# A tanh recurrence, attention and routed experts on one core: unused TensorE products at the start, chunk 0's steps on VectorE, and a planner that keeps the steps' rhythm

## The chip, the cores and the metric

The kernel runs on one core of one Trainium2 chip. A core has TensorE (matrix products, written to eight PSUM banks), VectorE, ScalarE and GpSimd, and a queue SP that only issues DMAs. In the profile they are PE (with PEld for loading weights), DVE, ACT, POOL and SP. Each engine takes its instructions in the order in which the program lists them, and waits on semaphores for the others. The metric is the device time of one execution in microseconds (us), lower is better, as a median over runs.

## The reference, cut to what matters

There are 4 sequences of 1024 tokens with 256 channels; all arithmetic is float32. A first block normalises the rows, makes two projections, and runs a recurrence along the tokens:

```python
px = x @ W_state.T + b_state;  g = sigmoid(x @ W_gate.T + b_gate)
state = tanh(p_t + state);  out_t = g_t * state        # one token after the other
x = x + layernorm(outs)
```

A second block normalises again, does causal attention with 16 heads of 16 channels (queries and keys RMS-normalised per head), adds it, RMS-normalises, picks the best two of four experts per token and adds their weighted outputs:

```python
attn = softmax(where(causal, q @ k.T * HD ** -0.5, -inf));  x = x + attn @ v @ wo.T
wts = top-2 of softmax(x_norm @ gate_w.T), renormalised
moe = wts[:, 0:1]*o0 + wts[:, 1:2]*o1 + wts[:, 2:3]*o2 + wts[:, 3:4]*o3
```

The block's result is normalised and added to x.

## The kernel before, in words

The tokens are cut into NI = 8 chunks of 128 tokens, each with all four sequences (B = 4). Per chunk there are these pieces of work:

- `inputs` (line 491) loads the rows into one of two buffers `xc`, on SP.
- `projections` normalises them (statistics in lines 448 and 449, the reciprocal root by `newton`, lines 432 to 439, or for chunk 0 by GpSimd's power in line 424; scaling in line 520), transposes them (line 462, copies from PSUM in line 471) and multiplies by the weights in four tiles of 128x512, eight products in line 533. VectorE evicts the tiles: states in line 551, halves of the gates in line 547.
- `recurrence` is one chain of 1024 steps for all chunks, 8 columns (2 halves of the channels x 4 sequences) wide. GpSimd adds the last state (line 582), ScalarE takes the tanh (line 585; line 578 for the very first).
- `gates` takes the tanh of the gates (line 566), after the chunk before has finished its steps.
- `before` multiplies gates and states in two parts, after step 96 and after step 128 (line 614), transposes (line 622), normalises, adds the input, stores it (line 651), normalises again and transposes; `heads` makes queries, keys and values (lines 710, 777, 797).
- Attention goes in tiles (i, b), chunk i and sequence b, with i + 1 blocks of keys for each of 16 heads: scores in two layouts (line 882), maxima on VectorE (line 974), exponentials on ScalarE (line 1023), masks on GpSimd (line 1043), sums (line 1064), output projection, and the router. It needs chunk i's recurrence, and grows with i.
- The experts follow when all tiles are done (lines 1504, 1523, 1564).

The order is written by a planner within the program. Each piece of work is a generator that yields an `Op` (engine, assumed cost, priority, events to wait for, slots, banks). `Plan.run` repeatedly takes the `Op` that can start first by its assumed clocks (ties by priority) and writes its instructions next on its engine. So the assumed costs (0.21 us for a sum and for a tanh) fix the order, and the chip then runs this order at its own pace. `projections` may go ahead for the first AT_ONCE = 5 chunks; later ones wait until the attention of chunk 0 is done. `once` holds the constants: memsets, masks, the scaling of weights by norms, zeros in DRAM. `fill` writes unused products (line 416) on TensorE wherever the plan has a gap of 0.8 us between 60 and 420 us of planned time.

Of the kernel before, what the change touches and what calls it, by code (L numbers as in the profile page):

```python
# [18 lines left out]
P = 128  # L19
# [23 lines left out]
def kernel(  # L43
# [42 lines left out]
    hb_g = const.tile([P, NCC], F32, name="hb_g")  # L86
    nc.vector.tensor_scalar_mul(hb_g, vec[:, 6:8], 0.5)

# [8 lines left out]
    for arena, group in (  # L97
# [18 lines left out]
    sandwich(  # L116
        tc, ident, mhalf, hb_g, route, keys, values,
        x, w_sg, w_qk, w_v, w_o, w_gate, row_d, weights, e_weights, out,
# [18 lines left out]

AT_ONCE = 5

# [31 lines left out]
class Op:  # L171
    def __init__(self, eng, cost, prio, reads=(), slots=(), banks=0, lag=0.0, either=(), ahead=0.0):
        self.eng, self.cost, self.prio, self.reads = eng, cost, prio, reads
        self.slots, self.banks, self.lag, self.either = slots, banks, lag, either
        self.ahead = ahead


class Plan:
# [7 lines left out]
    def __init__(self, banks):  # L186
# [4 lines left out]
        self.fill = None  # L191

    def ev(self, *key):
        return self.events.setdefault(key, Ready())

    def start(self, op):
        t = self.clock[op.eng]
        for r in op.reads:
            t = max(t, r.at + self.HOP)
        if op.either:  # L200
            t = max(t, min(r.at for r in op.either) + self.HOP)
        for s in op.slots:
            t = max(t, s.best()[1])
        for b in self.banks.pick(op.banks):
            t = max(t, self.banks.free[b])
        return t

# [11 lines left out]
    def run(self, streams):  # L219
        waiting = {}  # L220
        for n, s in enumerate(streams):
            op = next(s, None)
            if op is not None:
                waiting[n] = op
        while waiting:
            best = None
            for n, op in waiting.items():
                t = self.start(op)
                key = (t - op.ahead, op.prio, n)
                if best is None or key < best[0]:  # L230
                    best = (key, n, op, t)
            _, n, op, t = best
            assert t < float("inf"), "streams wait for each other"
            if op.eng == "PE" and op.cost and self.fill:
                self.fill(t)
            got = []
            for s in op.slots:
                k, _ = s.best()
                s.free[k] = float("inf")
                got.append((s, k))  # L240
            for b in self.banks.pick(op.banks):
                self.banks.free[b] = float("inf")
                got.append(b)
            self.clock[op.eng] = t + op.cost
            self.end = t + op.cost + op.lag
            try:
                waiting[n] = streams[n].send(got)
            except StopIteration:
                del waiting[n]
# [3 lines left out]
def sandwich(  # L253
    ctx, tc, ident, mhalf, hb_g, route, keys, values,
    x, w_sg, w_qk, w_v, w_o, w_gate, row_d, weights, e_weights, out,
# [75 lines left out]
    def once():  # L331

        yield Op("SP", 2.0, 50.0, [ev("x", 0)], lag=8.0)
        for t, ap in loads:
            nc.sync.dma_start(t, ap)
        done("loaded")
        yield Op("DVE", 2.0, 50.0, [ev("st", 0)])
        nc.vector.tensor_copy(ident_h, ident)
        nc.vector.memset(av, 0.0)
# [14 lines left out]
        for k in range(11):  # L354
# [3 lines left out]
            )  # L358
        for p in pads.tiles:
            yield Op("DVE", 1.2, 50.0)  # L360


            nc.vector.memset(p, 0.0)
            nc.vector.memset(p[:, 1, :, HD : HD + 1], 1.0)
        for cc in range(NCC):
# [10 lines left out]
        for e in range(1, E):  # L376
            nc.vector.memset(low[:, e, :e], 1.0)
            nc.vector.memset(nlow[:, e, :e], 0.0)
        yield Op("POOL", 1.5, -1.0)
        nc.gpsimd.memset(mask, 0.0)  # L380
        nc.gpsimd.affine_select(
            out=mask, in_=mask, pattern=[[-1, P]],
            compare_op=ALU.is_ge, fill=NEG, base=0, channel_multiplier=1,
        )
        nc.gpsimd.memset(late[:, : 3 * P], 0.0)

        nc.gpsimd.memset(earlier, 1.0)
# [5 lines left out]
        for k in range(KINDS):  # L393
# [8 lines left out]
            allow_small_or_imprecise_dtypes=True,  # L402
        )
        done("once")

    def fill(until):

        now = plan.clock["PE"]
        if not FILLED[0] <= now <= FILLED[1] or until - now < LEAST:
            return  # L410
        k, = banks.pick(1)
        if banks.free[k] > now:
            return
        n = int((until - now - 0.4) / 0.35)
        for _ in range(n):
            nc.tensor.matmul(banks.tiles[k], lhsT=ident_h, rhs=late, start=True, stop=True)
        banks.free[k] = max(banks.free[k], now + 0.35 * n)
# [9 lines left out]
    def newton(z, tag):  # L427

        n = z.shape[1]
        y = stat.tile([P, n], F32, tag=tag + "y", name=tag + "y", bufs=1)  # L430
        t = stat.tile([P, n], F32, tag=tag + "t", name=tag + "t", bufs=1)
        nc.vector.tensor_scalar(
            y.bitcast(I32), z.bitcast(I32), -0.5, float(0x5F3759DF), ALU.mult, ALU.add
        )
        nc.vector.tensor_scalar(z, z, -0.5, None, ALU.mult)
        for _ in range(3):
            nc.vector.tensor_tensor(t, y, y, ALU.mult)
            nc.vector.tensor_tensor(t, t, z, ALU.mult)
            nc.vector.scalar_tensor_tensor(y, t, 1.5, y, ALU.add, ALU.mult)
        return y  # L440

    def moments(prio, tiles, tag, reads):

        mv = stat.tile([P, len(tiles), 2], F32, tag=tag, name=tag)
        for n, t in enumerate(tiles):
            yield Op("DVE", 0.6, prio, reads)
            st6 = stat.tile([P, 6], F32, tag="st6", name="st6")
# [3 lines left out]

    def transposed(prio, srcs, reads, name, ahead=0.0):

# [13 lines left out]
        for cc, (eng, copy) in enumerate(  # L467
            (("ACT", nc.scalar.copy), ("DVE", nc.vector.tensor_copy))
        ):
            yield Op(eng, 0.65, prio, [ev(name, "in PSUM")])  # L470
            copy(to[:, cc, : n * P], banks.tiles[bs[cc]][:, : n * P])  # L471
            give(bs[cc])
# [7 lines left out]
    def states(i):  # L480

        both = keys.rearrange("p b (h t) -> p (b h) t", h=NHC)[:, :, i * P : (i + 1) * P]
        return both[:, : NCC * B, :], both[:, NCC * B :, :]

    def inputs():
# [9 lines left out]
    def projections():  # L495


        for i in range(NI):
            prio = 4.0 * i - 8.0
            while i not in xc_of:  # L500
                yield Op("DVE", 0.0, prio, [ev("x", i)])
            x_c = xcs.tiles[xc_of[i][1]]
            x_rows = [x_c[:, b, :] for b in range(B)]
            mv = yield from moments(
                prio, x_rows, "mv0", [ev("x", i), *([ev("av", B - 1)] if i >= AT_ONCE else [])]
            )
            done("mv0", i)
            z = stat.tile([P, B], F32, tag="z0", name="z0")
            if i:
                yield Op("DVE", 2.2, prio)  # L510
                nc.vector.tensor_scalar(z, mv[:, :, 1], LN_EPS, None, ALU.add)
                r = newton(z, "r0")
            else:
# [4 lines left out]
            for b in range(B):  # L518
                yield Op("DVE", 0.35, prio, [ev("r0", i)])
                nc.vector.tensor_scalar(  # L520
                    x_rows[b], x_rows[b], mv[:, b, 0:1], r[:, b : b + 1],
                    ALU.subtract, ALU.mult,
                )
            done("ln", i)
            to, lnT_ = yield from transposed(prio, x_rows, [ev("ln", i)], f"lnT{i}")
            give(xc_of[i])
            lnT = big.tiles[to[1]]
            st, g = states(i)
            for half, dc in ((0, 0), (0, 1), (1, 0), (1, 1)):
# [14 lines left out]
                pb = pb.rearrange("p (b t) -> p b t", b=B)  # L544
                yield Op("DVE", 0.68, prio, [ev("pp", i, half, dc)])
                if half:
                    nc.vector.tensor_scalar(
                        tile, pb, 0.5, hb_g[:, dc : dc + 1], ALU.mult, ALU.add
                    )
                else:  # L550
                    nc.vector.tensor_scalar(tile, pb, b_s[:, dc : dc + 1], None, ALU.add)
                give(pp)
                if (half, dc) == (0, 1):
                    done("st", i)
            done("half g", i)
# [13 lines left out]
    def recurrence():  # L569

        prev = None
        for i in range(NI):
            st, _ = states(i)
            last = ev("st", i)
            for t in range(P):
                if prev is None:
                    yield Op("ACT", 0.21, -9.0, [last])
                    nc.scalar.activation(st[:, :, t], st[:, :, t], AF.Tanh)
                else:
                    yield Op("POOL", 0.21, -9.0, [last])  # L580
                    s = sp.tile([P, NCC * B], F32, tag="s", name="s")
                    nc.gpsimd.tensor_tensor(s, st[:, :, t], prev, ALU.add)  # L582
                    done("s")
                    yield Op("ACT", 0.21, -9.0, [ev("s")])
                    nc.scalar.activation(st[:, :, t], s, AF.Tanh)  # L585
# [5 lines left out]
                if t == MOST - 1:  # L591
                    done("most", i)
            done("rec", i)


# [722 lines left out]
    def gate(pr, w, sm):  # L1318
# [31 lines left out]
    plan.run([  # L1350
        inputs(), projections(), gates(), once(), recurrence(), before(),
        *(heads(0, [b]) for b in range(B)), scores(), look_maxima(),
# [382 lines left out]
```

## Time and profile before

| | us |
|---|---|
| median of 3 runs (lowest, highest) | 1473.57 (1470.53, 1474.31) |
| the profiled execution's own time | 1475.52 |
| its span, first to last instruction | 1473.8 |
| PE busy | 1324.7 (90%) |
| DVE busy | 897.8 (61%) |
| ACT busy | 709.1 (48%) |
| POOL busy | 466.0 (32%) |

The profile is of one execution. A row of the timeline gives start, busy time, engine, line, operation, output and inputs with shapes, how many were merged, and in brackets the idle time of the engine before it and who ended it. A row of the stages gives a stretch of the span and, for every engine, its busy time and number of instructions in it, and the clock that TensorE was granted as a share of full speed. Line numbers below are those of the kernel before; the changed kernel's have shifted.

### The profile page before, as it was taken

Reading aid. Unit: us, or ns where it says so; the run is one execution under the profiler, and the core shown is the slowest. Engines: PE = TensorE matmul, PEld = TensorE weight load, DVE = VectorE, ACT = ScalarE, POOL = GpSimd, SP = SyncE. Lnnn points to the kernel's source line nnn. Section 1 sums busy time; section 2 is a strip of 40 time slices with the busy share of each in tenths; the row PEclk is TensorE's granted clock in tenths of the full one; section 3 lists DMA queues with packets and bytes.
Section 4 is the critical chain, followed back from the end, with each engine's and each line's share of the span. In section 5 each row is a group of like instructions: output and inputs, shape, how many; then the busy total and the mean of one; then the engine's idle time right before and its main releaser. Section 6 shows DMA issues by size and latency. Waiting matters only on the chain. (4 is left out here: it accounts for less than half of the span.)

```text
span 1473.8 us, 43265 instructions
## 1 busy us (share of the span) xinstructions
PE 1324.7 (90%) x17491; PEld 1032.5 (70%) x17506; DVE 897.8 (61%) x2725; ACT 709.1 (48%) x2144; POOL 466.0 (32%) x1466
## 2 busy tenths in 40 slices
PE   4578788998998999999999999999899999999994
PEld 2235446666676776787677677887688889888883
DVE  5566578599688788778877887783414312123331
ACT  2445555655765765776665455657122222223220
POOL 2433544534444444334311100111223312114221
PEclk8789899999999989998999999999899999999997
DMA  4010010001000010001000100221222110102100
GB/s 127 26 46 2 2 43 16 17 2 46 3 31 16 3 32 17 3 18 31 3 4 18 31 3 4 68 75 61 63 76 65 54 50 29 37 23 80 53 28 23
DMA packets 35847, 48.96 MB, mean 33 GB/s; under 512 B 7702, under 2 KB 27926, under 8 KB 35606
## 3 DMA queue, kind: packets, MB, share of 16 engines
q1 hardware_dynamic: 28774, 25.20, 5.5%
q0 software_dynamic: 6560, 20.09, 4.8%
q8 instruction: 143, 2.34, 0.7%
q14 instruction: 98, 0.80, 0.2%
q10 hardware_dynamic: 272, 0.52, 0.1%
HBM read 32.34 MB, written 13.73 MB: 31 GB/s over the span
## 5 line engine op out<-in xcount | busy, mean ns | idle before, releaser
L1023 ACT ACTIVATE ex<-bank 128x512 f32<-128x512 f32 (+1 forms) x592 | 326.2, 582 | 152.1 <-PE bank L882 87.2
L882 PE MATMUL bank<-keys,q 32*128 32x128 f32 x4608 | 352.7, 293 | 16.4 <-ACT q L761 3.6
L582 POOL TENSOR_TENSOR s<-keys 128x8 f32<-128x8 f32 x1023 | 223.1, 218 | 384.5 <-ACT keys L585 373.6
L882 PE MATMUL bank<-q,keys 32*128 32x128 f32 x4608 | 334.7, 293 | 6.5 <-ACT ex L1023 4.1
L882 PEld LDWEIGHTS bank<-q,keys 32*128 32x128 f32 x4608 | 273.7, 193 | 77.1 <-issue 42.9
L585 ACT ACTIVATE keys<-s 128x8 f32<-128x8 f32 x1023 | 218.5, 214 | 211.7 <-POOL s L582 209.1
L882 PEld LDWEIGHTS bank<-keys,q 32*128 32x128 f32 x4608 | 293.0, 193 | 35.9 <-DVE nm L974 6.0
L974 DVE TENSOR_REDUCE nm<-bank 128x1 f32<-128x512 f32 (+4 forms) x336 | 203.2, 639 | 51.4 <-PE bank L882 42.9
L967 DVE CUSTOM_DVE_ANT_0 bank<-bank,late 128x512 f32<-128x512 f32 (+2 forms) x320 | 188.4, 623 | 50.2 <-PE bank L882 49.0
L1043 POOL TENSOR_SCALAR_AFFINE_SELECT ex<-ex 128x256 f32<-128x256 f32 (+1 forms) x240 | 102.7, 429 | 261.6 <-ACT ex L1023 260.7
L1064 PE MATMUL av<-ex,values 128*17 128x128 f32 x4608 | 175.1, 282 | 2.2 <-DVE avT L1083 1.1
L1504 PE MATMUL bank<-values,keys 128*128 128x256 f32 x632 | 150.3, 385 | 6.2 <-PEq L1668 3.2
L1064 PEld LDWEIGHTS av<-ex,values 128*17 128x17 f32 x4608 | 110.0, 99 | 39.1 <-issue 15.2
L1504 PEld LDWEIGHTS bank<-values,keys 128*128 128x128 f32 x632 | 119.5, 193 | 23.8 <-issue 3.7
L1564 ACT ACTIVATE keys<-bank 128x256 f32<-128x256 f32 x136 | 52.2, 384 | 156.1 <-PE bank L1504 155.6
L1504 PE MATMUL bank<-keys 128*128 128x256 f32 x384 | 84.8, 379 | 0.0
L1504 PEld LDWEIGHTS bank<-keys 128*128 128x128 f32 x384 | 73.0, 190 | 9.9
L1591 DVE SCALAR_TENSOR_TENSOR rwnext<-av,rwnext 128x192 f32<-128x192 f32 x28 | 10.4, 414 | 101.6 <-PE av L1523 101.6
L533 PE MATMUL bank<-big,wsg 128*128 128x512 f32 x128 | 63.7, 643 | 5.9 <-ACT big L471 5.9
L710 PE MATMUL bank<-wqk,big 128*128 128x512 f32 x128 | 65.2, 638 | 3.2 <-ACT big L471 3.2
L1523 PE MATMUL av<-keys 128*128 128x192 f32 x384 | 66.4, 326 | 0.0
L1564 ACT ACTIVATE hid<-bank 128x256 f32<-128x256 f32 x66 | 25.4, 384 | 85.2 <-PE bank L1504 85.2
(238 smaller groups left out, 1720.2 us busy)
## 6 DMA issues: line engine op xcount, KB each, us to landing
row_d<-xn SPq DMA_DIRECT2D x16, 512.0 KB
xn<-in_x SPq DMA_DIRECT2D x8, 512.0 KB
xc<-in_x SPq DMA_DIRECT2D x7, 512.0 KB
keys<-in_e_l SPq DMA_DIRECT2D x2, 1024.0 KB
keys<-in_e_w SPq DMA_DIRECT2D x2, 512.0 KB
keys<-in_e_down SPq DMA_DIRECT2D x2, 384.0 KB
rwnext<-row_d,ids POOLq DMA_INDIRECT x36, 4.0
xc<-in_x SPq DMA_DIRECT2D x4, 128.0 KB
```

The costliest lines, as they stand in the source:

```text
L582: nc.gpsimd.tensor_tensor(s, st[:, :, t], prev, ALU.add)
L585: nc.scalar.activation(st[:, :, t], s, AF.Tanh)
L710: nc.tensor.matmul(pqk, lhsT=hT[:, cc, b * P : (b + 1) * P], rhs=wqk[:, cc, :], start=(cc == 0), stop=(cc == NCC - 1),)
L882: nc.tensor.matmul(banks.tiles[pbs[j]][:, m * P : (m + 1) * P], lhsT=k if kind == "sT" else q, rhs=q if kind == "sT" else k, start=(m == 0 ...
L967: nc.vector.tensor_tensor_reduce(out=s_, in0=s_, in1=late[:, 4 * P - w :], scale=-1.0, scalar=FMAX, op0=ALU.add, op1=ALU.min, accum_out=by ...
L974: nc.vector.tensor_reduce(by_slot[:, half, h0:h1, 2 * p + j], banks.tiles[pb][:, m0 * P : m1 * P].rearrange("p (h w) -> p h w", h=h1 - h0) ...
L1023: nc.scalar.activation(exs.tiles[ex[1]][:, j, : step.w], banks.tiles[pb][:, : step.w], AF.Exp)
L1043: nc.gpsimd.affine_select(out=d, in_=d, pattern=pattern, compare_op=ALU.is_ge, fill=0.0, base=0, channel_multiplier=-1,)
L1064: nc.tensor.matmul(av[32 * j : 32 * j + HD + 1, hc, :], lhsT=v_all[:, b, kb, 4 * hc + j, :], rhs=exs.tiles[ex[j // 2][1]][:, j % 2, m * P ...
L1504: nc.tensor.matmul(hb[0].tiles[hb[1]], lhsT=w[:, j, m * P : (m + 1) * P], rhs=src[:, j, :], start=(j == 0), stop=(j == nk - 1),)
L1523: nc.tensor.matmul(ob[0].tiles[ob[1]][:, t, :], lhsT=src[:, j, t * P : (t + 1) * P], rhs=w[:, j, :], start=(j == 0), stop=(j == nk - 1),)
L1564: nc.scalar.activation(to, src, AF.Gelu)
```

## The change

- At the start VectorE makes a bfloat16 identity, and TensorE multiplies it by itself BEFORE_ALL = 100 times into a bank that nobody reads, ahead of chunk 0's transposes.
- Chunk 0's two state tiles are evicted in two pieces each, the first 32 steps apart from the other 96. The first tanh waits for the first piece of the second tile.
- Chunk 0's sums (BY_VECTOR = 1) are done by VectorE instead of GpSimd.
- Projections of chunks 1 and 2 are cut into small VectorE instructions (`small`): statistics per 128 columns, scaling per 128 columns, copies and evictions of 128 columns, each an `Op` of its own. Chunks 3 and 4 no longer go ahead (AT_ONCE = 3).
- GpSimd writes the masks first, and the pads that VectorE cleared before.
- The planner's costs for a step are 0.24 (GpSimd) or 0.17 (VectorE) and 0.22 (ScalarE) instead of 0.21 and 0.21, and an `Op` that would delay the next step's `Op` on its engine is put behind it, unless it is too long for any gap and can start right behind the last step.

Cut to its core:

```diff
-AT_ONCE = 5
+SOONEST = 32
+BEFORE_ALL = 100
+BY_VECTOR = 1
+FITS = 0.05
+RIGHT_BEHIND = 0.06
+AT_ONCE = 3
...
+        if op.eng in self.chain and not op.every and op.cost:
+            ended, due, cost = self.chain[op.eng]
+            if t < due < t + op.cost - FITS and not (
+                op.cost > due - ended and t <= ended + RIGHT_BEHIND
+            ):
+                t = due + cost
         return t
...
+            if op.every:
+                self.chain[op.eng] = t + op.cost, t + op.every, op.cost
...
+    def begin():
+        yield Op("DVE", 0.2, -20.0)
+        nc.vector.tensor_copy(ident_h, ident)
+        done("ident")
+        pb, = yield Op("PE", 6.5, -20.0, [ev("ident")], banks=1)
+        for _ in range(BEFORE_ALL):
+            nc.tensor.matmul(
+                banks.tiles[pb][:, :P], lhsT=ident_h, rhs=ident_h, start=True, stop=True
+            )
+        give(pb)
+        yield Op("DVE", 0.2, -7.5, [ev("r0", 0)])
+        nc.vector.tensor_scalar_mul(hb_g, vec[:, 6:8], 0.5)
+        done("hb")
...
+            small = 0 < i < AT_ONCE
...
-                yield Op("DVE", 0.68, prio, [ev("pp", i, half, dc)])
...
+                pieces = [(slice(0, B), slice(0, P))]
+                if small:
+                    pieces = [(slice(b, b + 1), slice(0, P)) for b in range(B)]
+                elif i == 0 and not half:
+                    pieces = [(slice(0, B), slice(0, SOONEST)), (slice(0, B), slice(SOONEST, P))]
+                for k, (bs, ts) in enumerate(pieces):
+                    yield Op("DVE", 0.68 / len(pieces) + 0.05, prio, [ev("pp", i, half, dc)])
...
+                    if (half, dc, k) == (0, 1, 0):
+                        done("st", i)
...
-                    yield Op("POOL", 0.21, -9.0, [last])
+                    eng, name, cost = (
+                        (nc.vector, "DVE", 0.17) if i < BY_VECTOR else (nc.gpsimd, "POOL", 0.24)
+                    )
+                    step = 0.28 + cost
+                    if t == 0:
+                        plan.chain.clear()
+                    yield Op(name, cost, -9.0, [last], every=step)
                     s = sp.tile([P, NCC * B], F32, tag="s", name="s")
-                    nc.gpsimd.tensor_tensor(s, st[:, :, t], prev, ALU.add)
+                    eng.tensor_tensor(s, st[:, :, t], prev, ALU.add)
                     done("s")
-                    yield Op("ACT", 0.21, -9.0, [ev("s")])
+                    yield Op("ACT", 0.22, -9.0, [ev("s")], every=step)
...
-        for p in pads.tiles:
-            yield Op("DVE", 1.2, 50.0)
-            nc.vector.memset(p, 0.0)
-            nc.vector.memset(p[:, 1, :, HD : HD + 1], 1.0)
...
+        for p in pads.tiles:
+            yield Op("POOL", 1.6, 50.0, [ev("st", 0)])
+            nc.gpsimd.memset(p, 0.0)
+            nc.gpsimd.memset(p[:, 1, :, HD : HD + 1], 1.0)
```

## The prediction

> **What bounds the kernel now.** The page's table of 40 slices came first: TensorE is 90% busy over the span and low only in the first tenth and the last slice. Then busy time by stage, cut where each chunk's recurrence ends (line 622 starts 0.1 to 1.5 us behind that). Columns: stretch, length, busy time (count) of PE, PEld, DVE, ACT, POOL, granted clock, DMA share, GB/s.
>
> ```profile
> 17.90:88.60 70.70, 40.78 (x103) 18.71 (x102) 42.58 (x161) 29.38 (x132) 28.93 (x142) 0.76 0.11 34
> 88.60:171.80 83.20, 66.50 (x573) 40.45 (x580) 51.81 (x169) 45.73 (x171) 37.44 (x145) 0.89 0.06 17
> 171.80:247.30 75.50, 59.89 (x441) 39.10 (x445) 58.84 (x199) 40.02 (x160) 30.46 (x133) 0.93 0.10 29
> 247.30:340.30 93.00, 87.09 (x1240) 60.90 (x1239) 71.42 (x214) 57.25 (x204) 46.46 (x174) 0.98 0.06 19
> 740.60:1010.00 269.40, 262.75 (x6136) 208.45 (x6132) 212.49 (x574) 155.36 (x311) 33.81 (x78) 0.99 0.11 35
> 1010.00:1473.80 463.80, 427.72 (x2512) 381.72 (x2512) 130.80 (x414) 120.72 (x294) 117.39 (x142) 0.96 0.16 47
> ```
>
> The unused products of line 416 are part of this: 4.5, 12.7, 13.3 and 5.6 us in the first four stretches. Without them TensorE idles for 34.4 us of chunk 0's recurrence (70.7 - 40.8 + 4.5), 29.4 of chunk 1's, 28.9 of chunk 2's, 11.5 of chunk 3's, and only 6.6 of the 269 us behind 740. So up to about 247 us the recurrence sets the pace, after that TensorE. What comes out earlier by 247 reaches the end; what is saved later, mostly not.
>
> Then the start and one step of the recurrence, in the timeline (start, busy us, engine, line, operation).
>
> ```profile
> 9.58 2.29 PE L462 MATMUL bank<-ident,xc 128*128 128x128 f32 x8 [9.58 <-DVE xc L520]
> 12.71 0.34 PEld L533 LDWEIGHTS bank<-big,wsg 128*128 128x128 f32 x1 [0.52 <-DVE big L471]
> 13.56 0.34 PEld L533 LDWEIGHTS bank<-big,wsg 128*128 128x128 f32 x1 [0.52 <-issue]
> 14.20 0.19 PEld L533 LDWEIGHTS bank<-big,wsg 128*128 128x128 f32 x1 [0.29 <-issue]
> 14.62 0.19 PEld L533 LDWEIGHTS bank<-big,wsg 128*128 128x128 f32 x1 [0.24 <-issue]
> 16.54 0.75 DVE L551 TENSOR_SCALAR keys<-bank,vec 128x512 f32<-128x512 f32 x1 [0.97 <-PE bank L533]
> 17.33 0.22 ACT L578 ACTIVATE keys<-keys 128x8 f32<-128x8 f32 x1 [5.68 <-DVE keys L551]
> ```
>
> A pass of 512 columns takes 0.85 us up to 13.6 and 0.43 from 14.2: TensorE speeds up 4.2 us after its first instruction. The last two rows: eviction of the first states, then the first tanh.
>
> ```profile
> 18.37 0.21 ACT L585 ACTIVATE keys<-s 128x8 f32<-128x8 f32 x1 [0.31 <-POOL s L582]
> 18.66 0.20 POOL L582 TENSOR_TENSOR s<-keys 128x8 f32<-128x8 f32 x1 [0.32 <-ACT keys L585]
> 18.89 0.21 ACT L585 ACTIVATE keys<-s 128x8 f32<-128x8 f32 x1 [0.31 <-POOL s L582]
> ...
> 192.13 0.20 ACT L1190 ACTIVATE pr<-z 128x16 f32<-128x16 f32 x1
> 192.36 0.17 DVE L1321 TENSOR_REDUCE tot<-pr 128x4 f32<-128x16 f32 x1 [0.88 <-ACT pr L1190]
> ```
>
> A step by GpSimd is 0.525 us. The last pair prices a hand-over ScalarE to VectorE at 0.035; back it is 0.04 (16.54 + 0.75 to 17.33).
>
> **The change part by part**
>
> *Unused products before the rows.* They need line 534's cast (0.22, VectorE idle until 3.9), so from about 2.9. Price of one, not in the trace: from below, a quarter of a fill (17 of 512 columns in 3.83 us: 0.225 warm, 0.43 cold), so 0.056 warm and 0.107 cold; from above, the f32 transposes with their own weights, 1.09/8 = 0.136 warm and 2.29/8 = 0.286 cold. With 4.2 us cold, 100 take 7.6 us (39 cold, 61 warm) to 15.8 (15 and 85) and end between 10.5 and 18.7. Line 462 stands behind them and could start at 9.57. If nothing were late, the warm path from 9.57 would be: transposes paced by the four scalings to 10.7, copies to 11.35 and 11.95, two tiles of four 0.43 passes to 14.8, eviction, first tanh at 15.2 instead of 17.33. When TensorE is late, all rows are scaled and the first tanh follows 5.1 us behind the last product. I take 0.12 cold, 0.065 warm, near the lower end, since the fills show a load of 0.098 hidden completely: 35 cold and 65 warm, 8.4 us, end 11.3, first tanh 16.4: -0.9 (ends -1.7 and +6.5).
>
> The Trainium skill, TensorE: Matmul & The Clock Gate, section What you observe, has 107 ns for about the first 38 bf16 products and 56 after; by it 100 take 7.5 us, the first tanh comes at 15.5, and the sum would be 0.9 us lower.
>
> *First eviction in two pieces.* 0.17 (VectorE's price of four elements, rows of 128x4) + a quarter of 0.75 - 0.17 = 0.315 instead of 0.75, counted above. The rest (0.6) stands before the first sum: +0.3 below.
>
> *Chunk 0's sums by VectorE.* Step: 0.215 + 0.035 + 0.165 + 0.04 = 0.455, so 127 take 57.8. VectorE must now put all else between the sums. In the changed program's order 106 of the 126 gaps hold something, 93 a single small instruction. Its price isn't in the trace: line 448's 0.40 for 256 elements against 0.17 for four gives 0.285 for half a row; a quarter eviction 0.315. The gap is 0.29, and neighbours overlap by 0.08 (line 448 starts at 64.05, its predecessor ends at 64.13):
>
> ```profile
> 63.95 0.18 DVE L449 BATCH_NORM_AGGREGATE mv<-st 128x2 f32<-128x6 f32 x1
> 64.05 0.39 DVE L448 BATCH_NORM_STATS2 st<-xc 128x6 f32<-128x256 f32 x1
> ```
>
> So singles fit, at zero; from above, without overlap and at the full 0.40, a step is 0.165 + 0.04 + 0.40 + 0.04 = 0.645, and 93 x 0.19 = 17.7 us. The nearer row is the overlap. The larger gaps delay the sum, each by its length less 0.29: rest of the eviction 0.3; av, qn_s, listed and sq memsets (0.48 + 0.68 + 0.22 + 0.27) 1.36; two gate evictions 0.92; two groups of statistics 0.74; weights' scaling twice (0.87) 1.16; copies of three and two quarters 0.9; last memset group 0.5; line 697's 0.95, 0.66; two pairs of Newton steps 0.2: 6.7. On ScalarE four instructions of 0.6 delay by 0.36 each: 1.4. Total 57.8 + 8.1 = 65.9 instead of 70.7: -4.8 (ends -4.8 and +12.9).
>
> The skill's VectorE: DVE Perf Modes, section The TRN2 errata, speaks against the pieces: every instruction pays a fixed latency, so tiles of at least 512 are advised. The 0.17 agrees; if that latency were never overlapped, 0.285 + 0.04 against 0.29 adds 3.3 us and the sum loses two thirds of this gain.
>
> *Moved.* Chunk 3's projection leaves chunk 0's stretch for chunk 1's (the at-once chunks are three instead of five): TensorE 16 x 0.43 + 1.1 = 8.0, VectorE 9.5 (4 x 0.57, 2.1, 1.4, 0.7, 3.0), ScalarE 0.6. It costs nothing beside 29.4 us of idle TensorE and VectorE's 31.4 free; without that cover +8. Chunk 4's, at 79 to 107 before, follows it. The pads' memsets (4 x 0.98) go from VectorE to GpSimd, which has no sums then; they are due before line 710 at 110 and cost nothing. The masks go ahead of GpSimd's r at 7.7 (about 1 us from 2.6: nothing). On SP the input loads of chunks 5 and 6 move behind chunk 0's store (line 651) and the maxima's copies: each waits for the transposes of chunks 3 and 4, and chunk 1's store and copies queue behind it. Those transposes stand ahead of chunk 1's own on TensorE, so nothing is added; if they came late, chunk 1's path would shift by as much.
>
> *Planner's costs and alignment.* These only move instructions. For every step I added what stands between two tanhs (at row means, 0.58 for line 1023) above 0.31, or between two sums above 0.33, the larger: 13.6, 9.3 and 23.2 us in chunks 1 to 3 before; 67.2 + these is 80.8, 76.5 and 90.4 against 83.2, 75.5 and 93.0 measured. The changed order gives 12.8, 9.8 and 19.7: -0.8, +0.5, -3.5.
>
> **Sum.** -0.9 - 4.8 - 0.3 = -6.0 at 247, where TensorE becomes tight; of chunk 3's 3.5 I count 2.5, as 11.5 us of idle are left there. -8.5 from the profiled 1475.5 gives 1467.0; that execution was 1.95 above the median, so 1465.
>
> **Rivals.** *Nothing measurable (1472).* The lead is eaten: the changed interleaving in the tight stretch costs what was won, or the products end at the upper bound (+6.5 for -0.9). For it: TensorE's small waits after 300 (line 1090 for the copy of av, 7.4 us; line 797 for pads, 6.2) depend on order alone. Against it: the recurrence's lead is upstream of all.
> *Slower (1481).* A filler doesn't fit its gap. In chunk 0 each of 93 gaps overflows; below 0.065 us the gain stays positive (6.0/93), from 0.11 on the kernel is over 0.3% slower; at 0.17, near the upper bound of 0.19, 15.8 - 8.5 = +7. For it: half a row of work behind every sum, and VectorE already 60% busy there. Against it: the overlap above.
> *More (1454).* The planner knew steps of 0.48 where the trace has 0.525, so instructions were queued before their data; with 0.52 the waits named above and the 11.5 and 10 us of idle in chunks 3 and 4 shrink by half: another -11.
>
> **How the numbers follow.** Forecast 0.48 (its own range 1459 to 1469), more 0.11, nothing 0.18, slower 0.23. Forecast and more are faster by over 0.3% (4.4 us, about what a measurement here can tell): 0.59; same 0.18; slower 0.23. The range takes in "more" and the slower case up to a 0.19 overflow: 1452 to 1483.
>
> **What would show it.** First tanh near 16.4; adjacent tanhs of chunk 0 0.455 apart, and 0.455 also where a piece lies between two sums; chunk 0's recurrence about 66 us, line 705's starts near 83, 166 and 242; TensorE's idle from 250 on unchanged. Wrong if steps with a piece take 0.55 or more, if line 507 starts after 13, or if the lead at 250 doesn't reach 1010.

## The result and the profile after

The changed kernel takes 1479.67 us (median of 10 runs, 1473.64 to 1480.71) against 1473.38 us (10 runs, 1470.53 to 1476.54) for the kernel before on the same chip: a ratio of 1.0033, interval 1.0019 to 1.0047. It is slower by 0.33%; the forecast was faster by 0.6%. The profiled execution took 1479.93 us with a span of 1478.2.

The stages of the changed kernel, cut at the ends of chunk 0's, 1's and 2's recurrence, then the stretch from the last recurrence to the experts, then the experts. Columns as before: stretch, length, busy time (count) of PE, PEld, DVE, ACT, POOL, granted clock, DMA share, GB/s.

```profile
16.90:82.20 65.30, 33.33 (x92) 14.80 (x92) 48.49 (x274) 29.26 (x131) 0.42 (x1) 0.75 0.08 25
82.20:163.70 81.50, 65.72 (x585) 40.37 (x592) 53.46 (x178) 45.50 (x172) 37.94 (x145) 0.91 0.06 15
163.70:239.40 75.70, 64.29 (x499) 40.27 (x506) 64.56 (x215) 41.02 (x161) 31.75 (x137) 0.98 0.12 36
...
731.50:1048.80 317.30, 310.16 (x6820) 248.54 (x6815) 232.79 (x642) 177.90 (x361) 41.96 (x93) 0.96 0.11 34
1048.80:1478.20 429.40, 397.85 (x2002) 356.63 (x2001) 119.74 (x372) 102.97 (x255) 110.63 (x130) 0.97 0.16 47
```

And the last two of these stretches in the kernel before:

```profile
740.40:1043.60 303.20, 292.56 (x6652) 233.50 (x6645) 223.40 (x616) 173.03 (x349) 40.50 (x91) 0.98 0.11 35
1043.60:1473.80 430.20, 398.11 (x2001) 356.88 (x2001) 119.90 (x372) 103.20 (x255) 110.72 (x130) 0.97 0.17 47
```

The recurrence is ahead: chunk 0 takes 65.1 us from the second tanh instead of 70.7, chunk 2's ends at 239.4 instead of 247.3, the last at 731.5 instead of 740.4. Then the lead of 8.9 us turns into a lag: the experts start at 1048.8 instead of 1043.6, after 310.2 instead of 292.6 us of TensorE work behind the recurrence. The experts themselves take the same time. Two things are in these 17.6 us: more products (6820 instructions instead of 6652), and a lower granted clock (0.96 instead of 0.98). So TensorE had more of its work left at the end of the recurrence, although the recurrence was earlier, and did it more slowly.

Where that work was left is seen in the products of the projections, stage by stage. Columns: stretch, length, PE busy (count), PEld busy (count), granted clock, DMA share, GB/s. First the kernel before (its line 533), then the changed one (line 600). Sixteen instructions are one chunk.

```profile
0.00:17.90 17.90, 6.21 (x12) 2.89 (x13) 1.00 0.66 202
17.90:88.70 70.80, 27.87 (x53) 11.39 (x51) 0.76 0.11 35
88.70:171.80 83.10, 7.03 (x16) 3.04 (x16) 0.90 0.06 17
171.80:247.30 75.50, 7.52 (x16) 2.99 (x16) 0.93 0.10 29
247.30:340.30 93.00, 7.53 (x16) 2.73 (x16) 0.98 0.06 19
```

```profile
0.00:17.20 17.20, 4.76 (x11) 2.19 (x12) 1.00 0.64 211
17.20:82.30 65.10, 18.73 (x38) 7.73 (x36) 0.75 0.08 25
82.30:163.70 81.40, 0.00 (x0) 0.00 (x0) 0.91 0.06 15
163.70:239.40 75.70, 14.81 (x32) 6.00 (x32) 0.98 0.12 36
239.40:332.50 93.10, 7.63 (x16) 2.77 (x16) 0.93 0.09 25
```

Before: chunks 0 to 3 by the end of chunk 0's recurrence, then one chunk per stage; six chunks in all by 247. After: chunks 0 to 2, then *none* in chunk 1's stretch, then two in chunk 2's; five by 239. One projection, 7.5 us of products and 1.0 to 1.6 of transposes, has moved behind the point from which TensorE is tight. The reason is a wait, but not one for the whole attention of chunk 0, nor one of the chip: the planner gives out the statistics of chunks 3 and up when its clocks have the sums of chunk 0's fourth tile done (line 1147 of the changed kernel). That fixes their place in the order. On the chip chunk 3's first statistics even start before these sums; its scaling (line 585), its transposes (line 507) and the first of its products (line 600) follow as VectorE and TensorE reach them:

```profile
153.64 0.42 DVE L493 BATCH_NORM_STATS2 st<-xc 128x6 f32<-128x256 f32 x1
153.87 1.07 PE L1147 MATMUL av<-ex,values 128*17 128x128 f32 x32 [0.71 <-POOL s L664]
160.99 1.37 DVE L585 TENSOR_SCALAR xc<-xc,mv,r0y 128x256 f32<-128x256 f32 x4
161.62 1.56 PE L507 MATMUL bank<-ident,xc 128*128 128x128 f32 x8
168.35 1.02 PE L600 MATMUL bank<-big,wsg 128*128 128x512 f32 x2
```

Chunk 1's stretch ends at 163.7, so there was no room left in it. Its idle TensorE time stayed idle, or went to unused products (16.9 us of line 438 there, against 12.7 of line 416 before).

The smaller steps of the start came out near the forecast. The start of the changed kernel, in the timeline:

```profile
2.88 8.45 PE L538 MATMUL bank<-ident_h 128*128 128x128 bf16 x100 [2.88 <-DVE ident_h L534]
11.16 1.05 PE L507 MATMUL bank<-ident,xc 128*128 128x128 f32 x8
14.46 0.88 DVE L626 TENSOR_SCALAR keys<-bank,vec 128x128 f32<-128x128 f32 x2 [1.53 <-PE bank L600]
16.57 0.22 ACT L653 ACTIVATE keys<-keys 128x8 f32<-128x8 f32 x1 [4.18 <-DVE keys L626]
```

and two steps of chunk 0 with a piece of chunk 1's eviction between the sums:

```profile
41.53 0.17 DVE L664 TENSOR_TENSOR s<-keys 128x8 f32<-128x8 f32 x1
41.62 0.34 DVE L626 TENSOR_SCALAR keys<-bank,vec 128x128 f32<-128x128 f32 x1
41.74 0.22 ACT L667 ACTIVATE keys<-s 128x8 f32<-128x8 f32 x1 [0.24 <-DVE s L664]
41.99 0.18 DVE L664 TENSOR_TENSOR s<-keys 128x8 f32<-128x8 f32 x1
```

The sums are 0.46 apart with a piece of 0.34 in between: the piece starts 0.08 before the sum's end is recorded and ends as the next tanh does, so it delays nothing.

### The profile page after: what moved, and what is told of

The parts are those of the page before. It is cut to its first block, busy times and chain, and to the rows that moved or that the text cites. A ratio compares the mean times of both kernels' runs of the same rounds, so it can differ in the third digit from the quotient of the medians.

```text
span 1478.2 us, 43532 instructions
## 1 busy us (share of the span) xinstructions
PE 1341.7 (91%) x17601; PEld 1049.5 (71%) x17621; DVE 916.6 (62%) x2892; ACT 708.3 (48%) x2144; POOL 446.2 (30%) x1347
## 5 line engine op out<-in xcount | busy, mean ns | idle before, releaser
L965 PE MATMUL bank<-keys,q 32*128 32x128 f32 x4608 | 360.6, 297 | 17.7 <-ACT q L844 4.5
L965 PE MATMUL bank<-q,keys 32*128 32x128 f32 x4608 | 339.4, 294 | 5.9 <-ACT ex L1106 1.6
L965 PEld LDWEIGHTS bank<-q,keys 32*128 32x128 f32 x4608 | 277.1, 193 | 74.1 <-issue 38.7
L965 PEld LDWEIGHTS bank<-keys,q 32*128 32x128 f32 x4608 | 299.0, 196 | 38.5 <-DVE nm L1057 10.1
L664 POOL TENSOR_TENSOR s<-keys 128x8 f32<-128x8 f32 x896 | 198.8, 222 | 398.0 <-ACT keys L667 397.2
L1606 PEld LDWEIGHTS av<-keys 128*128 128x128 f32 x384 | 62.8, 190 | 0.6
```

What stands on the lines that cost most here:

```text
L664: eng.tensor_tensor(s, st[:, :, t], prev, ALU.add)
L965: nc.tensor.matmul(banks.tiles[pbs[j]][:, m * P : (m + 1) * P], lhsT=k if kind == "sT" else q, rhs=q if kind == "sT" else k, start=(m == 0 ...
L1606: nc.tensor.matmul(ob[0].tiles[ob[1]][:, t, :], lhsT=src[:, j, t * P : (t + 1) * P], rhs=w[:, j, :], start=(j == 0), stop=(j == nk - 1),)
```

## The experiments

Ratios are to the kernel before on the same chip; that kernel took 1473 to 1481 us on the chips used, so times of different runs are compared by ratio alone. Three theories stood at the start, A, B and C in the expectations. *Debt* (A): the loss is the projections that left chunk 0's stretch, and the rest of the change gains. *Clock* (B): useful work runs longer at a lower granted clock, whatever stands where. *Order* (C, later called scatter): any new order written by the planner moves the time by as much.

### How many chunks go ahead

```diff
-AT_ONCE = 3
+AT_ONCE = 5
-            small = 0 < i < AT_ONCE
+            small = 0 < i < 3
```

> The changed kernel with AT_ONCE 5 again, pieces only for chunks 1 and 2 as in the change. Theory A (debt): the change took the projections of chunks 3 and 4 out of chunk 0's recurrence, where TensorE is idle anyway; by the end of chunk 2's recurrence it had done 137.6 us of useful work instead of 149.5, so the lead of 7.9 us found 11.9 us more work behind it. With five at once that work is back in chunk 0's stretch: about 8 to 10 us less than the changed kernel's 1479.7, so 1470 or 1471, if chunk 0's steps are not held up by the unsplit pieces by more than 2 us. Theory B (clock): useful work runs longer at the half clock, whatever stands where: 1477 to 1481. Theory C (any new order moves the time by some us either way): no direction, 1470 to 1482.

Measured: 0.9926 (0.9903 to 0.9949), faster than the kernel before. The kernel before with AT_ONCE = 3:

> The kernel before with AT_ONCE 3 and nothing else. Theory A: the same debt without any lead, 8 to 12 us slower than before: 1481 to 1485. Theory B: the same as before within 2 us. Theory C: no direction, within 6 us of before.

Measured: 1.0110 (1.0075 to 1.0145). Four at once in the changed kernel (small pieces for chunks 1 and 2):

> The changed kernel with AT_ONCE 4: chunk 3's projection goes ahead again, chunk 4's doesn't. Theory A (debt): half of the difference between three and five at once, so about 0.998 of before, between the changed kernel (1.0033) and five at once (0.9926). Theory C (any new order moves the time): no direction; 0.99 to 1.01.

Measured: 0.9959 (0.9940 to 0.9978). Five at once, and all four of chunks 1 to 4 in small pieces:

> Five at once, and chunks 3 and 4 cut into small pieces too. Theory A: useful work by the end of chunk 2's recurrence as with five at once unsplit, and chunk 0's recurrence some 2 us shorter since no long instruction stands between the sums: 0.990 to 0.993 of before. If the pieces no longer find gaps (106 of 126 are filled in the change already), they come after chunk 0's recurrence, into its path to the heads, and it is slower than five at once unsplit: 0.995.

Measured: 0.9919 (0.9894 to 0.9943). In this order three instead of five cost 1.1% in both kernels (1.0110 to 1, 1.0033 to 0.9926), and four lie between. The direction is that of the debt theory; the size, 16 us, is above its 8 to 12. The count of products does not give the step from five to four: with four, too, 97 product instructions have run by the end of chunk 2's recurrence, as in the kernel before, but that end comes at 250.0 instead of 246.7. The rest of the change was worth -0.74%, or -11 us, where -8.5 had been forecast for the whole.

### The other parts

One unused product instead of 100 (99 products that nobody reads are left out):

```diff
-        for _ in range(BEFORE_ALL):
+        for _ in range(1):
```

> The changed kernel with 1 unused product at the start instead of 100; the order of all else is the same, since the planned cost is kept. All theories: the first tanh comes at about 16.7 to 17.2 instead of 16.57 (the cold passes come back, but the transposes start at 8.9), and the time stays within 1.5 us of the changed kernel's 1479.7. If the products themselves hold the start up, it is 1 to 2 us faster.

Measured: 1.0069 (1.0045 to 1.0093). The changed kernel once more, on the chip of the second group of runs:

> The changed kernel itself once more, so that it stands on one chip beside the others of this series. Both theories: 1.003 to 1.005 of the kernel before.

Measured: 1.0026 (1.0009 to 1.0043). The 100 products are thus worth 0.43%, uncertain by 0.3% (6 us). The start without them, in the timeline:

```profile
10.01 2.30 PE L507 MATMUL bank<-ident,xc 128*128 128x128 f32 x8 [6.83 <-DVE xc L585]
17.96 0.22 ACT L653 ACTIVATE keys<-keys 128x8 f32<-128x8 f32 x1 [5.89 <-DVE keys L626]
```

With them the transposes start later, at 11.16, take 1.05 instead of 2.30, and the first tanh is 1.4 us earlier (in the profile of the second execution of the changed kernel, 15.58, 2.4 us). In the execution without them the rows were also scaled 0.7 us later (from 9.54 instead of 8.83). The expectation, within 1.5 us of the changed kernel, was missed; what makes up the other 4 us was not tested.

Five at once, with chunk 0's sums on GpSimd (BY_VECTOR = 0):

> Five at once (0.9926) with chunk 0's sums by GpSimd again. A step takes 0.525 us instead of 0.457, so chunk 0's recurrence loses 127 x 0.068 = 8.6 us, and gains back the sums' waits behind VectorE's long instructions, 4 to 6 us. Theory A: 2 to 5 us slower than five at once, 0.994 to 0.996. If the step's length on VectorE were all that counts: 8.6 us slower, 0.998.

Measured: 0.9947 (0.9928 to 0.9966). Chunk 2's recurrence ends 3.9 us later than with VectorE (250.6 to 246.7), and the time is 0.21% (3 us, uncertain by 4) longer. Five at once, without the rule that puts an `Op` behind the next step:

```diff
-        if op.eng in self.chain and not op.every and op.cost:
+        if False and op.eng in self.chain and not op.every and op.cost:
```

> Five at once (0.9926) without the planner's rule that puts other work behind the next step of the chain; costs as in the change. If the rule is worth what my walk along the order gave in chunks 1 to 3 (3.8 us in all) plus what it protects in chunk 0 on VectorE: 4 to 8 us slower, 0.995 to 0.998. If it does nothing on the chip: within 2 us of five at once.

Measured: 1.0028 (1.0008 to 1.0048), 1.0% above five at once and more than expected. Chunk 0 then takes 83.4 us, and its timeline shows what the rule keeps out, pairs of pieces between two sums:

```profile
33.81 0.16 DVE L664 TENSOR_TENSOR s<-keys 128x8 f32<-128x8 f32 x1
33.89 0.60 DVE L626 TENSOR_SCALAR keys<-bank,vec 128x128 f32<-128x128 f32 x2
34.01 0.21 ACT L667 ACTIVATE keys<-s 128x8 f32<-128x8 f32 x1 [1.45 <-DVE s L664]
34.41 0.16 DVE L664 TENSOR_TENSOR s<-keys 128x8 f32<-128x8 f32 x1
```

With two pieces of 0.34 the next sum comes after 0.60 instead of 0.46. Here, too, a delay early on reaches the end: chunk 2's recurrence ends 15.9 us later than with the rule, and the kernel takes 15 us more (1.0028 - 0.9926). Both delays come out at about their full size. But these two runs do not have the same work in the same stages as five at once: by the end of chunk 2's recurrence 114 and 113 product instructions have run, against 100, nearly a projection more. By the debt theory's reckoning that should have won some of the delay back.

Unused products for longer, to keep the clock up:

```diff
-FILLED = (60.0, 420.0)
+FILLED = (60.0, 1000.0)
```

> The changed kernel with planned gaps on TensorE filled by unused products up to 1000 us of planned time instead of 420; three at once. Theory B (clock): between 250 and 1040 us the changed kernel spent 79 us of its first profile at half clock and 65 in its second, which cost 37 and 29 us of useful work; if filling keeps the clock up, half of that time goes and it is 6 to 12 us faster than the changed kernel: 0.995 to 0.999 of before. Theory A (debt): the lead and the debt are as before, the products fill idle time only: 1.001 to 1.004.

Measured: 1.0024 (1.0003 to 1.0045), the same as the changed kernel. The mean granted clock of ten runs rose from 0.947 to 0.955, but line 438 took 60.4 us of TensorE until the experts instead of 42.6. In the profiled execution what the clock gave went mostly into these products and idle time: from the end of chunk 2's recurrence to the experts TensorE's useful time is 740.1 us instead of 760.3, idle time and unused products are 64.7 instead of 49.1. The 0.995 to 0.999 of the clock theory was missed.

### Other orders of the same work

The planner's HOP is the time that it assumes for a hand-over between engines. Another value changes the order of instructions, and with it the number of unused products, which fill planned gaps: with HOP at 0.025, 0.03 and 0.035 the profiles have 124, 139 and 163 in the kernel before and 168, 149 and 153 in the changed one. More of them go with a longer time in the first and a shorter one in the second, so their number does not explain the differences below. All else is the same work.

```diff
-    HOP = 0.03
+    HOP = 0.035
```

> The changed kernel with the planner's assumed hand-over 0.035 us instead of 0.03: a slightly different order of everything, the same work, and the same chunks at once. Theory A: the debt is the same, 1477 to 1482. Theory C: the time moves by several us, to anywhere between 1468 and 1488.

Measured: 0.9976 (0.9955 to 0.9997): the changed kernel becomes 0.6% faster by an order alone.

> The kernel before with the planner's assumed hand-over 0.035 us instead of 0.03: another order of the same work. Theory A: within 3 us of before (0.998 to 1.002). Theory C: up to 8 us either way.

Measured: 1.0056 (1.0039 to 1.0072): the kernel before becomes 0.6% slower. The order theory is right as far as this. Five at once in this order:

> Five at once (unsplit chunks 3 and 4) in the order that the planner makes with a hand-over of 0.035 us. The changed kernel in this order was at 0.9976 of before. Theory A (debt): the difference between three and five at once stays in another order: 0.988 to 0.993. Theory C (the order alone): no fixed difference; 0.99 to 1.006.

Measured: 0.9992 (0.9976 to 1.0007), no better than three (0.9976). With that the debt theory had failed in one order, and it did so again in three of the runs that follow. So the rest of the table was run: three and five, before and changed, with HOP at 0.025, on one chip, and the missing cell at 0.035.

> The kernel before with the planner's hand-over at 0.025 us instead of 0.03: the same instructions in another order. Debt theory (the loss comes from projections 3 and 4 that left chunk 0's stretch): near the kernel before, within 0.6% either way as the order at 0.035 was (1.0056), so 0.994 to 1.006. Scatter theory (the order alone makes the differences): the same; this run is the reference for the three others in this order.

Measured: 0.9972 (0.9951 to 0.9993).

> The kernel before with only three chunks at once, hand-over 0.025. Debt theory: about 1.0% slower than the kernel before in the same order (the first order gave 1.0110), at least 0.5%. Scatter theory: as often faster as slower, between -0.6% and +0.6% of it.

Measured: 0.9983 (0.9967 to 0.9999).

> The changed kernel, hand-over 0.025. Debt theory: 0.5 to 1.0% slower than the same with five chunks at once in this order. Scatter theory: within 0.6% of it, either sign. Against the kernel before both allow 0.997 to 1.008.

Measured: 0.9963 (0.9947 to 0.9978).

> The changed kernel with five chunks at once (small pieces for chunks 1 and 2 as in the change), hand-over 0.025. Debt theory: 0.990 to 0.996 of the kernel before, and 0.5 to 1.0% below the changed kernel in this order. Scatter theory: 0.990 to 1.002, with no fixed distance to the three others.

Measured: 0.9922 (0.9893 to 0.9951), in microseconds 1463.45, the lowest median of all.

> The kernel before with three chunks at once, hand-over 0.035; five at once in this order gave 1.0056. Debt theory: 0.5 to 1.0% slower than that, 1.011 to 1.016. Scatter theory: 1.000 to 1.011.

Measured: 1.0059 (1.0040 to 1.0077).

> The changed kernel with five at once, all four ahead-going chunks in small pieces, hand-over 0.035; with 0.03 it was the best version, 0.9919. Debt theory: below the changed kernel in this order (0.9976), at 0.990 to 0.996. Scatter theory: 0.992 to 1.003, as the one with whole pieces in this order (0.9992).

Measured: 0.9972 (0.9952 to 0.9992).

| HOP | before (five) | before, three | changed (three) | changed, five | change as made | five kept | three for five: before, changed |
|---|---|---|---|---|---|---|---|
| 0.025 | 0.9972 | 0.9983 | 0.9963 | 0.9922 | -0.09% | -0.50% | +0.11%, +0.41% |
| 0.03 | 1 | 1.0110 | 1.0033 | 0.9926 | +0.33% | -0.74% | +1.10%, +1.08% |
| 0.035 | 1.0056 | 1.0059 | 0.9976 | 0.9992 | -0.80% | -0.64% | +0.03%, -0.16% |

The last three columns compare within a row, and are each uncertain by about 0.3%. What follows:

- With five chunks kept ahead the change gains in every order, 0.5 to 0.7% (7 to 11 us).
- Three for five costs 0.43% (6 us) on the mean of the six pairs, but from nothing to 1.1% by the order; three orders are too few to tell this mean from nothing. The displaced projection is there in all six: by the end of chunk 2's recurrence 81 or 85 product instructions have run with three, 97 to 101 with five. That it is displaced is shown; what it costs depends on the order.
- The change as made is slower in one order of three. The order alone moves one and the same kernel by 0.7 to 0.8% (from 0.9972 to 1.0056 before, from 0.9963 to 1.0033 changed).

The pair on one chip at 0.025, changed with three, then with five, shows the displacement most plainly (projection products from the start of the recurrence to the end of chunk 2's, columns as above):

```profile
17.00:81.90 64.90, 18.66 (x38) 7.70 (x36) 0.75 0.08 25
81.90:163.30 81.40, 0.00 (x0) 0.00 (x0) 0.91 0.06 15
163.30:243.20 79.90, 15.74 (x32) 6.49 (x32) 0.96 0.12 34
```

```profile
16.40:87.10 70.70, 25.04 (x46) 10.14 (x44) 0.76 0.11 31
87.10:168.80 81.70, 11.23 (x25) 4.25 (x24) 0.92 0.08 21
168.80:244.70 75.90, 7.70 (x16) 2.87 (x16) 0.89 0.11 29
```

In these two executions the recurrence with three is ahead by 5.2 us at the end of chunk 0 and by 1.5 at the end of chunk 2, and the experts start 1.1 us later (1038.0 and 1036.9): the lead bought nothing.

What stays open is why the price of the displaced projection goes from nothing to 1.1% between orders. The granted clock has a part in it: the mean over the runs was 0.935 for the kernel before with three against 0.947 for the kernel before on that chip, 0.947 for both at 0.025, and 0.942 and 0.943 at 0.035; over the ten runs of the changed kernel, 0.01 less clock goes with 5.7 us more. By that rate 0.012 is some 7 of the 16 us.

The profiles show it too. From the end of chunk 2's recurrence to the end of the last, then to the experts, the changed kernel with three, first with HOP at 0.03, then at 0.025 (columns as for the stages):

```profile
239.40:731.40 492.00, 456.51 (x7498) 337.61 (x7506) 391.24 (x1195) 309.45 (x1063) 214.13 (x810) 0.94 0.06 18
731.40:1048.80 317.40, 310.26 (x6824) 248.64 (x6816) 232.89 (x642) 178.00 (x362) 41.96 (x93) 0.96 0.11 34
```

```profile
243.20:720.80 477.60, 445.16 (x7350) 329.10 (x7355) 388.08 (x1191) 305.20 (x1057) 213.19 (x811) 0.96 0.06 18
720.80:1038.00 317.20, 309.12 (x6966) 246.96 (x6966) 235.02 (x642) 180.90 (x368) 42.06 (x94) 0.97 0.11 34
```

Both have the same products there (48 instructions of projections and 8704 of scores in each), yet without the unused ones (6.5 and 11.4 us) TensorE took 760.3 us for them in the first and 742.9 in the second. The clock records of the traces have it at half clock for 85 us of this time in the first, 57 in the second, and 63 in the kernel before. The clock does not explain every pair: the kernel before at 0.025 spent less time there at half clock with three (62 us) than with five (68), and took longer for its products (751.6 to 736.0). Why one order brings more slow time than another was not found.

## Why the prediction was wrong

*The step that failed* is "Moved": "Chunk 3's projection leaves chunk 0's stretch for chunk 1's ... It costs nothing beside 29.4 us of idle TensorE ...; without that cover +8." The cover did not exist. Chunk 1's stretch ends at 163.7, and the planner's wait put chunk 3's transposes at 161.6 and its products from 168 on. The count of projection products by stage shows none in chunk 1's stretch, two chunks in chunk 2's, and one chunk fewer by 247. The wait stood in the description of the kernel; its time could have been read in the trace of before, where chunk 5 is the first that waits for the same: its statistics begin at 166, its products at 204, long after the end of chunk 1's recurrence at 171.8.

```profile
166.31 0.42 DVE L448 BATCH_NORM_STATS2 st<-xc 128x6 f32<-128x256 f32 x1
204.18 1.88 PE L533 MATMUL bank<-big,wsg 128*128 128x512 f32 x4
```

The term, put at 0, was +16 us in the order measured (three for five, 1.08%). From the end of chunk 2's recurrence to the experts TensorE's useful time grew by 17.5 us over the kernel before (742.8 to 760.3). About 8.8 of them are the displaced projection itself (products 23.1 us instead of 15.1, transposes 3.1 instead of 2.3), as large as the +8 named for the case without cover. The rest is no further product but slower ones, with 85 us at half clock instead of 63; the prediction had no term for that. In the other orders the cover was missing as well, and the term came out between -2 and +6 us. So the missing cover is shown, and what three for five cost in this order; what sets that price stays open.

*The measure of the lead* failed with it: "What comes out earlier by 247 reaches the end." Here the recurrence was 7.9 us earlier at that point, TensorE was one projection of 8 to 9 us behind, and then ran slower. Without the alignment rule and with GpSimd's sums a delay did reach the end (15 us for 15.9 and 3 for 3.9, each uncertain by 4), but with more projections done by then than in the run they are compared with; that the two agree so well is in part luck.

*Unused products*: forecast first tanh 16.4, measured 16.57 in the first profile and 15.58 on another chip. The end of the products was right (11.3), by two errors that cancel: 35 cold ones at 0.12 were taken, 54 at 0.107 and 45 at 0.056 came (below). The gain of "-0.9" was too small: without them the kernel is 0.4% slower.

*First eviction in two pieces*: the first tanh starts 0.39 us after the first piece (16.18 to 16.57); 0.315 + 0.04 had been forecast.

*Chunk 0's sums by VectorE*: forecast 0.455 per step and 65.9 us; measured 0.46 and 65.1 us from the second tanh to the end. The singles fit at no cost where rows were looked at, and the upper bound did not come. The Trainium skill, VectorE: DVE Perf Modes, section The TRN2 errata, warns of the fixed latency of small tiles; these rows show part of it overlapped, since a piece starts 0.08 us before the sum ahead of it is recorded as ended. With five at once chunk 0 still takes 70.4 us; with chunks 3 and 4 in small pieces too it takes 65.8, so the likely reason is their unsplit instructions between the sums.

*Planner's costs and alignment*: -0.8, +0.5, -3.5 was forecast for chunks 1 to 3 as they follow from the order; measured -1.7, +0.2 and +0.1. Chunk 3's saving did not come; that the projections which moved near it are the cause was not tested. The alignment rule itself is worth 1.0% with five at once.

*The sum*: -8.5 was forecast; with five at once the change measured -7, -11 and -9 us in the three orders. So the sum held in size for the change without AT_ONCE = 3, and in this order the miss is as large as that one term. That the rest came out near the forecast is partly luck: its own terms did not. The unused products measured 6 us for 0.9 (with three chunks ahead), VectorE's sums 3 for 4.8, and the alignment rule alone 15 for the 2.8 of costs and alignment together; these were taken out one at a time, so they do not add up.

*The rivals*: "Nothing measurable" had the right place (the interleaving in the tight stretch eats the lead), but put its price at the lead's size; in this order it was twice that. "Slower" gave a time near the measured one by the wrong mechanism: chunk 0's recurrence was 5.6 us shorter, so its fillers did not overflow their gaps on the whole. (Its bounds mix two sums: 0.065 and 0.11 us are worked out from the 6.0 us at 247, the +7 from 8.5; from 8.5 they would be 0.09 and 0.14.) "More" fell: from chunk 2's end to the experts TensorE's idle time with the unused products was 53.5 us before (length 796.3 - busy 751.1 + unused 8.3) and 49.1 after (809.4 - 766.8 + 6.5), not half. That another order of the same work moves the time by 0.7 to 0.8% had no term of its own in the forecast; in the order at 0.035 the change as made was in fact 0.8% faster.

## What to carry to other kernels

When work that fills one engine's idle time is moved, look up the last event that its new place waits for, and compare that time with the end of the idle stretch: idle time that lies before the event is no cover. A lead on a critical chain need not reach the end; compare the bounding engine's useful work at the same point, not only the time of the point, and look at what clock it does the rest. And where a planner writes the order, price a change in several orders of the same work before believing half a per cent either way.

## What had not been expected of the hardware

TensorE's change of speed came at different times. The 100 products of one chip's execution, then of another's (changed kernel, and the same with five at once), cut where the gap between starts falls from 107 to 56 ns; columns as for the projections (a product that reaches over the cut is counted on both sides):

```profile
2.80:8.60 5.80, 5.72 (x55) 5.73 (x56) 1.00 0.96 334
8.60:11.15 2.55, 2.55 (x49) 2.55 (x46) 1.00 0.61 186
```

```profile
2.80:5.70 2.90, 2.82 (x27) 2.82 (x28) 1.00 1.01 356
5.70:9.80 4.10, 4.10 (x76) 4.10 (x73) 1.00 0.97 328
```

The slow phase lasted 5.7 us in the one and 2.8 in the other; in thirteen executions with these products, between 2.8 and 5.7. That is up to 1.4 us of the first tanh, by nothing in the program: the changed kernel itself had 5.7 on one chip and 3.6 on another. The column of the granted clock says 1.00 in both phases, so this slow start is seen only in durations. The Trainium skill, TensorE: Matmul & The Clock Gate, section What you observe, has the same two gaps, 107 and 56 ns, and a change around 4 us with 0.5 us of spread; the gaps agree with these rows, the spread here was larger.
